# Layer 0 of a two-layer block: shift weights loaded first, the gate turned within the first group, a rotary product ahead of the turns, and all experts' inputs turned first at the end

## The chip, the cores and the metric

The kernel runs on one core of one Trainium2 chip. Its time is the device time of one execution in microseconds (us), as the median of several runs. A profile is one further execution, recorded by the hardware. The core has five engines, each with an instruction queue of its own that is worked off in order: TensorE (PE) for matrix products and transposes, VectorE (DVE), ScalarE (ACT), GpSimd (POOL), and SyncE (SP), which here only issues DMA transfers. POOL and ACT issue a few transfers too. PEld in the profile is the loading of TensorE's stationary operand.

## The reference

Two transformer layers with adaptive layer norm over 1024 tokens of width 512, all in float32. In layer 0 the vector `c` gives six rows by one product, `silu(c) @ wmod`: shift, scale and gate for the attention (rows 0, 1, 2) and for the feed-forward part (3, 4, 5). Attention has 32 query heads and 8 key/value heads of width 128, and its weights come as integers with scales:

```python
mod = (_silu(L0_c) @ L0_wmod).reshape(L0_c.shape[0], 6, 1, -1)
ga = (2 * (ga >= 0) - 1) * jnp.maximum(jnp.abs(ga), 0.25)
h = _layernorm(x, axis=-1) * (1 + ca) + sa
x = x + ga * _L0_attn_ref(h, scales_q, ..., qw_o)
...
w = (qw.astype(jnp.float32) - ZERO) * jnp.repeat(scales, GS, axis=0)
q = _apply_rope(q, cos, sin); k = _apply_rope(k, cos, sin)
scores = jnp.einsum('bhqd,bhkd->bhqk', q, k) / math.sqrt(HD)   # causal, softmax
```

A gated feed-forward part with low-rank additions follows. Layer 1 has its own modulation, attention with 32 heads of width 16, and at the end a mixture of 28 rank-8 experts: each token's two best experts by `logits = xf @ gate_W.T` are weighted by a softmax, and their low-rank outputs are added to a dense product.

```python
h = jnp.einsum('nd,erd->ner', xf, lora_A) * (gate_full * SCALING)[:, :, None]
out = xf @ base_W.T + jnp.einsum('ner,eor->no', h, lora_B)
```

## The kernel before

Everything before layer 1, and the kernel's end, is written in a manual schedule: on each engine the instructions stand in the order in which the Python code issues them. Semaphores between engines come from the tiles that an instruction reads and writes. A tile pool has a fixed number of buffers, and an instruction that needs a buffer waits until the one that held it before is through.

**The begin** (lines 428 to 557). SP issues the loads in the order written: `cc` (c as a column), `row` (c broadcast to all partitions), four tiles of `x`, four tiles of scale weights (`wm`), four tiles of shift weights (`wa`, lines 435 to 438), then the first key weights (`wi`, `ws`) and so on. Transfers of 256 KB each are the rule. DVE makes the layer norm's statistics (L444, L445), ACT the root of the variance (`rstd`, L447) behind the Sigmoid of `cc` (L484) and of `row` (L487). DVE multiplies `row` by its Sigmoid (L489), normalizes x to `xn` (L455) and sums the scale by one pass per chunk (`mod_sum`, L135). TensorE multiplies `cc` by `wa` to get the shift as a row (L497), then transposes `xn` (L465) and the row (L505); DVE copies the shift to `mcol` (L507), and DVE and ACT evict the normalized chunks to `hT` (L478, L473).

Then come the projections of key group 0 and of query heads 0 to 3: `project_k`, `project_v` and `project_q`. The rotary step `project_rope` has eight TensorE passes (L219), three DVE products (L225, L227, L228) and one addition on POOL (L232). `ready` dequantizes a loaded weight on DVE (L212), `load` issues the next one's two transfers on SP (L253, L254). Amid these stand the four `mod_sum` passes of the gate and, at the last one, four small steps that clamp it (L141 to L145). The last thing before the group loop is `gate_row`: DVE spreads the gate's column (L150), TensorE turns it (L158), one engine copies it to a row (L83).

Before the loop, products use four PSUM banks, two of `psA[0]` and two of `psA[1]`, and transposes four of `trp`. At `first.close()` all but `psA[0]` go to the scores' pool `sp`, three buffers of two banks. From there on `psum_mm` has two banks.

**The group loop** (lines 624 to 685). Eight groups, and in each eight steps over query tiles in the order 3, 7, 2, 6, 1, 5, 0, 4. A step `u` has four blocks of 32 queries for its four heads. `scores(u, s)` multiplies (L331), masks (L335, L337), takes the maximum (L339) and the exponential on ACT (L341); `normalize` takes the reciprocal (L348) and scales on ACT (L350). `turn_probs(u, b)` turns block b on DVE (L355) and sends four transfers to `pT` (L357), of blocks 0 and 2 from SP, of 1 and 3 from POOL. Block 0 is turned at the end of the step, blocks 1 to 3 in the following step. `context` and `project_o` (L366, L377) of a step run two steps later, as does `residual`, which multiplies by the gate row (L385). `plan` hands each step of group 0 the next group's products as side pieces; `exchange` dequantizes and loads.

**The end** (lines 1408 to 1423). For the last four token tiles: logits, routing on DVE, then steps given as a string: `b` is the dense product of a tile (L1273, eight passes), `t` weights a tile's expert inputs on DVE (`hg`, L1255) and turns them on TensorE (L1263, L1264), with two copies on ACT, and `e` adds the experts' product (L1280, L1281), multiplies by the gate and adds x on DVE (L1283, L1284) and sends the output. Banks come from a pool of seven, `hg` has two buffers, `hgT` five.

## Time and profile before

| | us |
|---|---|
| median of 3 runs | 1865.36 |
| lowest, highest | 1863.69, 1867.35 |
| profiled execution | 1870.42 |
| its span, first to last instruction | 1868.3 |
| PE busy | 1801.9 (96%) |
| DVE busy | 1164.4 (62%) |
| ACT busy | 671.9 (36%) |
| POOL busy | 479.1 (26%) |
| mean granted clock of TensorE | 0.983 |

All times within the profile count from the span's start. A line of a timeline gives start, length, engine, source line, operation, the tile written and the tiles read, the shapes and the number of instructions merged into it; in brackets, how long the engine was idle before and what ended that. A line of the waits gives engine, tile and line, what was waited for, then the total in us, how often, and the longest. In the profile's slices the span is cut into 40 equal parts, and a digit is the busy share in tenths. A line of the stretches gives the stretch, its length, then for PE, PEld, DVE, ACT and POOL the busy time with the number of instructions, and last the granted share of TensorE's clock, the DMA share and GB/s. Matmuls are pipelined and their ends are modelled, so times of single passes are best read from the distance between starts.

### The profile page before, as it was taken

How to read it: one execution, taken by the hardware profiler on the slowest of the kernel's cores; microseconds unless marked ns; L12 is line 12 of the kernel's file. 1: busy time of each engine (PE TensorE's matmuls, PEld its weight loads, DVE VectorE, ACT ScalarE, POOL GpSimd, SP SyncE). 2: the span in 40 equal slices, each digit the busy share in tenths (PEclk: the TensorE clock that was granted, in tenths of full speed). 3: DMA queues.
4: the chain of work that ended last, by engine and by line, in shares of the span. 5: the costliest groups of instructions: out<-in, count | busy, mean ns of one | idle time of the engine just before them, and what ended most of it. 6: DMA issues, size and time to landing. Idle time of an engine off the chain costs nothing.

```text
span 1868.3 us, 22566 instructions
## 1 busy us (share of the span) xinstructions
PE 1801.9 (96%) x6578; PEld 839.3 (45%) x6578; DVE 1164.4 (62%) x2823; ACT 671.9 (36%) x1398; POOL 479.1 (26%) x705
## 2 busy tenths in 40 slices
PE   7989999999999999999999999999999999999998
PEld 4444445444455444455444544444534433333434
DVE  5677685676765767766777772232555777576443
ACT  1144533434434444433435530000114334455531
POOL 1244443444433444433444420001100100000000
PEclk9999999999999999999999999999999989999999
DMA  6154453354543544533545551001000002000000
GB/s 220 56 150 130 126 143 95 92 146 120 137 115 83 131 120 119 158 91 103 134 108 147 144 193 60 0 0 51 1 2 7 6 11 72 4 8 5 8 18 34
DMA packets 87738, 156.39 MB, mean 84 GB/s; under 512 B 25264, under 2 KB 33072, under 8 KB 87616
## 3 DMA queue, kind: packets, MB, share of 16 engines
q1 hardware_dynamic: 70064, 117.00, 21.9%
q0 software_dynamic: 17312, 37.54, 8.4%
q8 instruction: 54, 0.88, 0.2%
q14 instruction: 68, 0.56, 0.1%
q10 hardware_dynamic: 240, 0.41, 0.1%
HBM read 74.90 MB, written 2.36 MB: 41 GB/s over the span
## 4 chain that ended last, share of the span: by engine, by line
PE 71%; DVE 14%; issue 6%; ACT 4%; DMA 2%; POOL 2%; SPq 1%; ACTq 0%; DVEq 0%; POOLq 0%
PE mm L366 9%; PE sc L823 8%; PE sc L331 8%; PE mm L219 7%; PE mm L377 7%; PE sc L1086 6%; PE sc L1039 5%; PE sc L855 4%; PE ctx L1129 4%; DVE pr L355 3%; PE mm L299 3%; PE sc L942 2%; ACT pr L341 2%; ACT pr L350 2%; DVE t L228 2%
## 5 line engine op out<-in xcount | busy, mean ns | idle before, releaser
L341 ACT ACTIVATE pr<-sc,nb 128x512 f32<-128x512 f32 (+7 forms) x256 | 189.1, 739 | 508.6 <-DVE nb L339 390.6
L219 PE MATMUL mm<-hT,wf 128*128 128x512 f32 x640 | 294.1, 604 | 10.2 <-DVE t L228 7.3
L357 POOL DMA_DIRECT2D pT<-pr x509 | 251.1, 500 | 146.9 <-DMA pT<-pr 43.1
L331 PE MATMUL sc<-kT,qT 128*128 128x512 f32 (+15 forms) x768 | 264.3, 468 | 3.8 <-ACT pr L341 3.0
L366 PE MATMUL mm<-pT,v 128*128 128x512 f32 x576 | 258.8, 594 | 2.8 <-DVE gu L585 1.6
L355 DVE STREAM_TRANSPOSE pr<-pr 128x512 f32<-128x512 f32 (+7 forms) x256 | 189.2, 760 | 82.4 <-ACT pr L350 75.7
L377 PE MATMUL mm<-wo,ctxT 128*128 128x512 f32 x512 | 230.7, 593 | 2.5 <-ACT ctxT L372 1.4
L1086 PE MATMUL sc<-q,kv 32*128 32x512 f32 (+3 forms) x768 | 212.0, 556 | 7.2 <-DVE mx L1049 7.2
L331 PEld LDWEIGHTS sc<-kT,qT 128*128 128x128 f32 x768 | 142.1, 191 | 160.1 <-issue 144.5
L350 ACT ACTIVATE pr<-pr,rs 128x512 f32<-128x512 f32 (+7 forms) x256 | 190.8, 765 | 8.3 <-DVE rs L348 8.3
L219 PEld LDWEIGHTS mm<-hT,wf 128*128 128x128 f32 x640 | 120.1, 193 | 149.4 <-issue 123.0
L339 DVE TENSOR_REDUCE nb<-sc 128x1 f32<-128x416 f32 (+31 forms) x256 | 181.1, 708 | 8.8
L1102 ACT ACTIVATE pspace<-sc 128x512 f32<-128x512 f32 (+3 forms) x303 | 132.3, 495 | 150.0 <-PE sc L1095 110.9
L1039 PE MATMUL sc<-kv,q 32*128 32x512 f32 (+3 forms) x768 | 171.7, 547 | 6.2 <-ACT kv L994 3.0
L386 POOL TENSOR_TENSOR x<-x,ot 128x512 f32<-128x512 f32 x62 | 78.5, 1265 | 345.8 <-DVE ot L385 271.3
L366 PEld LDWEIGHTS mm<-pT,v 128*128 128x128 f32 x576 | 107.7, 190 | 122.0 <-issue 113.3
L1049 DVE CUSTOM_DVE_ANT_0 q<-sc,cwide 128x128 f32<-128x128 f32 (+3 forms) x256 | 125.6, 491 | 52.3 <-PE sc L1039 28.2
L823 PE MATMUL sc<-hT,gu 128*128 128x512 f32 x352 | 153.3, 594 | 0.9 <-DVE ot L385 0.9
L377 PEld LDWEIGHTS mm<-wo,ctxT 128*128 128x128 f32 x512 | 95.9, 190 | 109.1 <-issue 100.9
L1086 PEld LDWEIGHTS sc<-q,kv 32*128 32x128 f32 x768 | 76.8, 191 | 96.4 <-ACT pspace L1102 33.9
L232 POOL TENSOR_TENSOR qT<-t,t 128x512 f32<-128x512 f32 x64 | 86.7, 1355 | 112.1 <-DVE t L228 111.7
L823 PEld LDWEIGHTS sc<-hT,gu 128*128 128x128 f32 x352 | 66.1, 190 | 86.4 <-issue 81.6
(195 smaller groups left out, 1831.2 us busy)
## 6 DMA issues: line engine op xcount, KB each, us to landing
wm<-in_wmodT_dram SPq DMA_DIRECT2D x44, 256.0 KB
wi<-in_qw_q_dram SPq DMA_DIRECT2D x32, 256.0 KB
ws<-in_s_q_dram SPq DMA_DIRECT2D x32, 256.0 KB
wi<-in_qw_o_dram SPq DMA_DIRECT2D x32, 256.0 KB
ws<-in_s_o_dram SPq DMA_DIRECT2D x32, 256.0 KB
pT<-pr SPq DMA_DIRECT2D x64, 128.0 KB
pT<-pr POOLq DMA_DIRECT2D x64, 128.0 KB, 3.2
pT<-pr SPq DMA_DIRECT2D x64, 112.0 KB
```

The costliest lines, as they stand in the source:

```text
L219: nc.tensor.matmul(ps, lhsT=wf[:, c, :], rhs=hT[half][:, c, :], start=(c == 0), stop=(c == NC - 1),)
L331: nc.tensor.matmul(ps[:, n0 : n0 + w], lhsT=q, rhs=kT[u.g][:, n0 : n0 + w], start=True, stop=True)
L339: nc.vector.tensor_reduce(nb, ps[:, : d0 + B], AX.X, ALU.max, negate=True)
L341: nc.scalar.activation(u.pr[:, :, :, s, :].rearrange("p j k i -> p k j i"), ps[:, :nk].rearrange("p (k j i) -> p k j i", j=NB, i=B), AF.Ex ...
L350: nc.scalar.activation(pr, pr, AF.Copy, scale=u.rs[s])
L355: nc.vector.transpose(t, t)
L357: queues[(REP * b + r) % len(queues)].dma_start(u.pT[b * B : (b + 1) * B, r, :, :, :].rearrange("p k s i -> p (k s i)"), t[r * B : (r + 1) ...
L366: nc.tensor.matmul(ps, lhsT=vv[u.g][:, kj, :], rhs=u.pT[:, :, kj, :, :], start=(kj == 0), stop=(kj == u.n - 1),)
L377: nc.tensor.matmul(ps, lhsT=u.ctxT[:, r, :], rhs=wo[u.g][:, r, :], start=(r == 0), stop=(r == REP - 1),)
L823: nc.tensor.matmul(ps, lhsT=w[:, m, c, :], rhs=hTc[b][:, c, :], start=(c == 0), stop=(c == NC - 1),)
L1039: nc.tensor.matmul(ps[:, at : at + w], lhsT=u.q[kp, bass.ts(i, P)], rhs=kT1[kp, u.g, n0 : n0 + w], start=True, stop=True,)
L1086: nc.tensor.matmul(ps[:, : QW - q0], lhsT=kT1[kp, u.g, bass.ts(kb, P)], rhs=u.q[kp, q0:QW], start=True, stop=kb < 4 * u.Q,)
```

## The change

In the begin, the four loads of shift weights are issued ahead of x, and `row` behind x. The last two gate sums and the clamp move behind the last query product; the query products go in the order q(2,0), q(3,0), q(2,1), q(3,1), and the dequantization of q3 with the load of q5 ahead of them. The gate's row is no longer made before the loop. Its column is spread at the end of step (0, 0), into a buffer of the loop's own pool, and turned and copied in step (0, 1), in a bank of `psum_mm`. Step (0, 1) does not turn its block 0 at its end: step (0, 2) does that, together with block 1, behind its first side piece, which is the product and rotary step of head 5's first half. At the kernel's end all four turns stand ahead of all four expert products.

```diff
         nc.sync.dma_start(cc, a["c0"])
-        row = const.tile([P, D], F32, tag="crow", name="crow")
-        nc.sync.dma_start(row, a["crow0"].partition_broadcast(P))
-        load_x(0)
-        scales = [mod_load(0, 1, c) for c in range(NC)]
         wa = []
         for k in range(NC):
             wa.append(fp.tile([P, D], F32, tag=f"wa{k}", name=f"wa{k}"))
             nc.sync.dma_start(wa[k], a["wmodS"][bass.ts(k, P), :])
+        load_x(0)
+        row = const.tile([P, D], F32, tag="crow", name="crow")
+        nc.sync.dma_start(row, a["crow0"].partition_broadcast(P))
+        scales = [mod_load(0, 1, c) for c in range(NC)]
...
             mod_sum(0, 2, c, gate[c])
-        project_q(2, 0)
         ready("q", 3)
         load("q", 5)
-        for c in range(2, NC):
-            mod_sum(0, 2, c, gate[c])
+        project_q(2, 0)
+        project_q(3, 0)
         project_q(2, 1)
-        project_q(3, 0)
         ready("k", 1)
         load("o", 0, 0)
         project_q(3, 1)
-        gate_row(0, 2, lambda: trp.tile([P, 512], F32, tag="tr", name="tr"))
+        for c in range(2, NC):
+            mod_sum(0, 2, c, gate[c])
         first.close()
...
+        spread = []
...
-                turn_prev(1)
-                piece()
+                if (g, i) == (0, 2):
+                    piece()
+                    turn_prev(0)
+                    turn_prev(1)
+                else:
+                    turn_prev(1)
+                    piece()
                 scores(u, 1)
+                if (g, i) == (0, 1):
+                    gate_row(0, 2, psum_mm, spread[0])
                 normalize(u, 0)
...
-                for b in range(NB if (g, i) == (NKV - 2, NT - 1) else 1):
+                if (g, i) == (0, 0):
+                    spread.append(gate_spread(0, 2))
+                for b in range(NB if (g, i) == (NKV - 2, NT - 1) else 0 if (g, i) == (0, 1) else 1):
                     turn_probs(u, b, queues)
...
-    for step in "b4 b5 t4 b6 t5 e4 b7 t6 e5 t7 e6 e7".split():
+    for step in "b4 b5 t4 b6 t5 t6 b7 t7 e4 e5 e6 e7".split():
```

## The prediction

> **What bounds the kernel now.** I read the page first: TensorE (PE) is busy 96% of the span, and its low tenths stand only at both ends, which are what the change touches.

> ```profile
> PE   7989999999999999999999999999999999999998
> PEclk9999999999999999999999999999999989999999
> ```

> Next, what PE waits for in the first 220 us. Four waits carry it: 12.3 us for the shift weights, 3.4 and 0.8 us around the gate row, 5.5 us for a rotary product's last DVE step.

> ```profile
> PE mm L497 <- DMA wa<-in_wmodS_dram: 12.3, 1, 12.3
> PE mm L219 <- DVE t L228: 5.9, 2, 5.5
> PE tr L158 <- DVE spread L150: 3.4, 1, 3.4
> PE sc L331 <- ACT gate L83: 0.8, 1, 0.8
> PE mm L219 <- DVE wf L212: 0.5, 1, 0.5
> ```

> Third, the timeline of the begin: PE's first product starts when wa lands, runs at half rate (6.57 us, eight passes, where eight later take 3.43), and holds the transposes until 18.77. DVE was through with xn at 13.4 and with the scales at 15.8.

> ```profile
> 6.05 0.63 ACT L487 ACTIVATE rsig<-crow 128x512 f32<-128x512 f32 x1 [3.43 <-DMA crow<-in_crow_dram]
> 6.74 2.35 SPq L438 DMA_DIRECT2D wa<-in_wmodS_dram  x4
> 12.28 6.57 PE L497 MATMUL mm<-wa,cc 128*1 128x512 f32 x8 [12.28 <-DMA wa<-in_wmodS_dram]
> ```

> Fourth, the timeline of the end: the last turn's DVE step (hg) stands behind expert 5's output (eo), PE idles 1.81 us, and what follows runs at half rate (0.85 us a pass instead of 0.43).

> ```profile
> 1856.94 0.69 DVE L1284 TENSOR_TENSOR eo<-eo,x 128x512 f32<-128x512 f32 x1
> 1857.55 0.39 DVE L1255 TENSOR_TENSOR hg<-ha,oh 128x224 f32<-128x224 f32 x1
> 1857.99 0.43 PE L1263 MATMUL sc<-ident,hg 128*128 128x128 f32 x1 [1.81 <-DVE hg L1255]
> ```

> Last, granted clock (third figure from the right) by 2 us stretches: each idle spell is followed by 3 to 7 us at 0.50.

> ```profile
> 80.00:82.00 2.00, 2.00 (x3) 0.76 (x3) 0.93 (x3) 0.18 (x1) 0.00 (x0) 0.50 0.00 0
> 84.00:86.00 2.00, 2.00 (x7) 0.91 (x6) 0.51 (x1) 0.00 (x0) 0.00 (x0) 1.00 0.00 0
> ...
> 120.00:122.00 2.00, 2.00 (x3) 0.67 (x2) 2.00 (x3) 1.14 (x4) 0.39 (x1) 0.50 0.35 109
> ```

> Between these places PE runs without a break (22.8 to 59.2, 80.6 to 112.9, 118.6 to 162), so a gain made early is kept.

> **The change, part by part**

> **Load order.** No bytes are added. SP keeps eight transfers in flight: from 6.05 us on one of 256 KB lands each 0.68 us (crow 6.05, x 6.72 to 8.76, wm 9.42 to 11.47, wa 12.14 to 14.17). If the slow first landing belongs to the start, not to crow, the new order lands wa at 6.05 to 8.1, x at 8.8 to 10.8, crow at 11.5, wm at 12.1 to 14.2. PE's first product then ends near 12.5 and leaves the path. But ACT's Sigmoid of crow stands ahead of the layer norm's root: 11.5 + 0.63 + table load 1.28 + 0.30 gives rstd at 13.7 (10.4 before). Then on DVE the reciprocal 0.2, four xn at 0.48: 15.9; four mod_sums at 0.62: 18.4; then the copy of the shift, which was at 21.11. The first projection starts 2.7 us earlier, at 20.05. If crow was what made the first landing slow (an isolated 256 KB row load, 46.50 to 49.11, took 2.6 us), all is up to 2.4 us earlier: 5.1. Against this, PE now idles from the transposes (about 16.8) to 20.05, and every spell of 1.8 us or more in this trace cooled the clock; half rate for 3.4 us costs 1.7. Bounds -1 to +5; I take **+1.5**, nearest to the row with the cold start taken off. Up to 59.18 PE has no other wait.

> **Gate into group 0, products reordered** (times as before, less the start's gain). DVE: rotary of q(1,1) to 61.4, two mod_sums to 63.78 (the second 1.75 because POOL's add runs beside it), dequant of q3 to 64.5. PE idles 62.6 to 64.55, then q(3,0), q(2,1), q(3,1) at 3.44 each: 74.9. DVE: rotaries at 2.1 behind each, the last to 77.05, then the two mod_sums (0.69 + 1.75 less overlap) and four small steps at 0.2: 80.1; now the first scores' mask and maximum (0.95): 81.1, where before they ended at 81.8. PE no longer waits for the gate: scores at 74.9 instead of 78.92, project_k(1,0) by 79.3 instead of 85.4 (0.50 clock). So DVE takes its rotary at 81.1, not 85.5, and the row-for-row rest of step (0,0) reaches its turn at 91.4 instead of 95.47: **4.05**. The spread copy (0.43) fits in DVE's 1.06 us wait for ACT before that turn. The four gate transposes cost 0.45 warm; their copy (0.58) on ACT is beside DVE work. They take one of the two "mm" banks, so q(4,1) must wait for the rotary of q(4,0), to 96.2: PE idles 2.1 us, but DVE wants q(4,1) only at 102.4.

> Moved DMAs: q5's load is issued 2 us earlier, with nothing behind it on SP; o(0,0) still follows k1's dequant. Hidden.

> **The product ahead of the turns.** Before, in (0,2), DVE waited until 113.31 for ACT, turned twice (to 116.6), then did q(5,0)'s rotary, to 118.57, for which PE's q(5,1) waited. After (less 4.05): scores' maximum to 108.0, rotary to 110.05 in what were idle 1.26 + 1.91 us, turns to 112.5. PE runs q(5,1) at 110.1 (118.62 before). Then project_o waits for wo's dequant behind the other turns: 117.05 to 120.5, before 125.67 to 129.1. The sum of both parts is **8.4** at that point. POOL's add now precedes block 1's four pT issues: it ends near 111.8, the turn at 112.5, so nothing waits. SP's four issues of block 0 come after the rotary: by SP's 1.07 us each the eight end near 120, land by 122.5; context(0,1) wants them at 123.4. That cover is 0.9 us; without it PE waits that much.

> Less cooling: new PE idles of 1.9, 2.1 and 3.05 us. The clock's records in the trace change only on a grid of 3.41 us; steps of it that were 45% busy (the end) and 18% busy (before 76.3) cooled the clock, one 69% busy did not. So an idle cools if over 1.88 us of it fall into one step: by where the grid may fall about 0.45, 0.5 and 0.8. A spell costs 1.7 to 3.4; less what DVE's slack hides I take 2.2, 0.7 and 2.0: 1.0 + 0.3 + 1.6 = 2.9. Bounds 0 and 7 (all three, two steps in the first and last); **+5.5** remains.

> [...]

> **The end.** Same instructions. Turn 5 ends at 1849.08; hg6 needs only turn 4 (done 1845.4), so t6 0.22, b7 3.43, t7 0.22: 1852.95; four experts at 1.72: 1859.8, before 1863.56. DVE's 1.4 us an expert is covered by PE's 1.72 until the last, whose tail is the same. **+3.7**: 1.8 of idling, 1.9 of cold clock. Bounds 1.8 (the clock cools elsewhere) and 3.8. What was eo ahead of hg is now later by 3.8 for e4; only its output transfer follows.

> **Sum.** 1.5 + 5.5 + 3.7 = 10.7. Against the profiled execution (1870.42, span 1868.3): 1859.7. That one lies 5.1 above the median, 1865.36; on the median 10.7 off gives **1854.7**.

> **The rivals**

> *No cooling in the new gaps.* 2.7 + 8.4 + 3.7 = 14.8: 1850.6. For it: the gaps are each under the grid's step. Against: 1856 to 1858. [...] Chance 0.17.

> *The begin gives nothing.* Crow's Sigmoid holds rstd longer or the clock stays cold for two steps: -1 instead of 1.5, 1857.2. For it: crow is now ninth of the big loads; against: scales still end by 18.4. Chance 0.15.

> *Group 0 gives its lead back* to the pT transfers (PE waited 0.45 us for one at 162): only the end counts, 1861.7. Against: the turns that feed them move as early as PE does. Chance 0.11.

> *Slower:* the clock's records have six half-rate stretches in layer 1, from 1397 to 1619, 44 us in all, which cost 22. A shifted program meets the grid otherwise; each further 3.41 us window costs 1.7, so from 7 more on the gain is gone; at nine, 1870.0. For it: these stretches follow short idles that may fall either way. Against: the three runs, each with its own grid, lie within 3.7 us. Chance 0.07.

> **How the numbers follow.** Likeliest 0.50 (own range 1851 to 1858), then 0.17, 0.15, 0.11, 0.07. Faster by over 0.2% (under 1861.6; about what a measurement can tell) is 0.50 + 0.17 + 0.15 and 0.04 of the fourth: 0.86; the fourth's rest and 0.02 of the last: 0.09 same; 0.05 slower. The range 1849 to 1862 leaves out the last case and the far end of the second.

> **What would show it.** Right: L497 starting before 7 us, rstd near 13.7, the first L219 near 20; no PE wait for spread or gate; q(5,1) without the 5.5 us wait; the end's PE unbroken from 1831 to the last expert. Wrong: crow landing after 14, a PE wait for hg or for a bank at t7, long 0.50 clock from 94 to 125, or more half-rate stretches in layer 1.

## The result and the profile after

| | before | after |
|---|---|---|
| median, us (14 executions each) | 1865.87 | 1857.26 |
| lowest, highest | 1858.21, 1870.6 | 1849.93, 1864.84 |
| profiled execution, us | 1870.42 | 1857.40 |
| its span | 1868.3 | 1855.3 |
| mean granted clock | 0.983 | 0.984 |

The changed kernel takes 0.9954 of the time before, 95% interval 0.994 to 0.9969: 8.6 us less (5.8 to 11.2). The two profiled executions differ by 13.0 us. That is not the size of the change: executions of one and the same kernel spread over 12 to 15 us. This spread goes with the clock: in the 14 executions of after the mean granted clock runs from 0.980 in the longest to 0.988 in the shortest, and time and clock correlate at -0.98 (-0.93 to -0.98 in every other group of nine or more executions). Which waits move the clock is part of what follows.

After the change, lines behind line 430 of the kernel carry numbers up to 9 higher: hg is L1264, its turn L1272 and L1273, the experts' product L1289 and L1290.

TensorE's slices and clock on the page of after:

```profile
PE   7989999999999999999999999999989999999998
PEclk8999999999999999999999999999999999999999
```

What PE waits for in the first 220 us of after (engine, tile and line, what it waited for, total in us, how often, longest):

```profile
PE mm L497 <- DMA wa<-in_wmodS_dram: 4.1, 1, 4.1
PE tr L465 <- DVE xn L455: 4.0, 1, 4.0
PE mm L366 <- DVE nb L339: 3.5, 1, 3.5
PE mm L219 <- DVE t L228: 2.3, 2, 1.9
PE mm L219 <- DVE wf L212: 1.8, 1, 1.8
PE mm L219 <- DVE hT L478: 1.7, 1, 1.7
```

Of the four waits of before, the 12.3 us for wa are down to 4.1, and the others are gone (3.4 and 0.8 at the gate's row, 5.5 for t). New ones stand elsewhere: 4.0 before the transposes, 1.8 for the dequantized q3 (wf), 1.9 for a bank (t), and 3.5 in front of a context product (L366). The timeline of PE in after shows where they lie:

```profile
4.12 6.33 PE L497 MATMUL mm<-wa,cc 128*1 128x512 f32 x8 [4.12 <-DMA wa<-in_wmodS_dram]
14.40 3.65 PE L465 MATMUL tr<-ident,xn 128*128 128x128 f32 x16 [3.96 <-DVE xn L455]
20.25 5.19 PE L219 MATMUL mm<-hT,wf 128*128 128x512 f32 x8 [1.69 <-DVE hT L478]
...
95.21 3.70 PE L219 MATMUL mm<-hT,wf 128*128 128x512 f32 x8 [1.87 <-DVE t L228]
...
109.16 3.70 PE L219 MATMUL mm<-hT,wf 128*128 128x512 f32 x8
...
114.13 3.70 PE L377 MATMUL mm<-wo,ctxT 128*128 128x512 f32 x8 [0.62 <-ACT ctxT L372]
...
124.03 7.10 PE L366 MATMUL mm<-pT,v 128*128 128x512 f32 x16 [3.46 <-DVE nb L339]
```

The first projection starts at 20.25 (22.77 before) and then takes 5.19 us instead of 3.67: it runs partly at half rate (granted clock 0.79 from 20 to 28 us). The product of head 5's second half, which waited for the rotary step of the first, runs at 109.16 (118.62 before). At 124.03 PE starts on the context of step (0,1), 0.87 us behind the landing of its last transfer of pT at 123.16. In all eight profiles with the product ahead, this distance is 0.83 to 0.87 us; so it is the transfer that the 3.46 us of idling belong to. The name nb is only that of the release seen last: in three of the eight, PE starts before the nb step at that place has ended. These are issues of pT on SP and the last ones on POOL, and from the view of the tile pT the shortest, median and longest time from issue to landing:

```profile
110.41 5.64 SPq L357 DMA_DIRECT2D pT<-pr  x8
...
115.02 1.93 POOL L357 DMA_DIRECT2D pT<-pr  x4 [1.01 <-DVE pr L355]
...
DMA to landing us min/median/max: 1.8/2.7/6.7
```

The end on PE's timeline of after has no wait for hg, and one expert's two halves take 1.02 us each:

```profile
1843.32 0.27 PE L1272 MATMUL sc<-ident,hg 128*128 128x128 f32 x1
1843.53 1.02 PE L1289 MATMUL sc<-eb,hgT 128*128 128x512 f32 x2
...
1849.56 1.02 PE L1290 MATMUL sc<-eb,hgT 96*128 96x512 f32 x2
```

**The lead.** To see where the time went, each of TensorE's passes is matched with the pass of the same place in the trace of before. The difference of the two starts is the lead there, in us. All leads below are against the one trace of before. "Begin" is the first projections, "gate" the mean over the passes at 89 to 95 us of after, where the lead falls from 6.6 to 4.1 at the wait for the bank, "ahead" those just before the context of (0,1), "context" those just behind it.

| profile | begin (56 us) | gate | ahead | context | end of layer 0 | start of layer 1 | 1740 us | 1834 us | span |
|---|---|---|---|---|---|---|---|---|---|
| after | 1.01 | 5.63 | 11.28 | 7.58 | 8.30 | 8.16 | 10.96 | 9.26 | 13.0 |
| after, again | -0.57 | 4.07 | 9.23 | 4.43 | 4.76 | 4.99 | 7.86 | 6.16 | 9.8 |
| end alone | 1.01 | 1.86 | 1.82 | 1.82 | 2.19 | 2.52 | 12.33 | 12.32 | 16.0 |
| begin alone | 2.59 | 3.45 | 3.44 | 3.44 | 3.59 | 3.62 | 6.12 | 1.48 | 3.2 |
| gate alone | 0.98 | 5.62 | 5.14 | 5.14 | 5.35 | 4.59 | 7.44 | 5.74 | 5.7 |
| product ahead alone | 0.23 | 0.17 | 6.27 | 3.01 | 3.19 | 3.33 | 6.05 | 1.55 | 3.2 |

Three things are read from it. The kernels with the old begin (rows 3, 5, 6) also have up to 1.0 us there, so a lead of 1 us at 56 us is no gain. Between the start of layer 1 and 1834 us no instruction differs in any of these kernels, and yet the lead moves by -2.1 to +9.8 us there. And the last column less the one before it is what the end gave: 3.6 to 3.7 with the new end; with the old one 0 in gate alone, and 1.7 in begin alone and in product ahead alone.

### The profile page after: what moved, and what is told of

Same layout as the page of the kernel before. It is cut to its first block, busy times and chain, and to the rows that moved or that the text cites. A ratio compares the mean times of both kernels' runs of the same rounds, so it can differ in the third digit from the quotient of the medians.

```text
span 1855.3 us, 22570 instructions
## 1 busy us (share of the span) xinstructions
PE 1798.5 (97%) x6578; PEld 838.6 (45%) x6578; DVE 1163.8 (63%) x2823; ACT 671.3 (36%) x1398; POOL 478.8 (26%) x705
## 4 chain that ended last, share of the span: by engine, by line
PE 72%; DVE 15%; ACT 5%; issue 5%; DMA 2%; POOL 1%; SPq 1%; ACTq 0%; DVEq 0%; POOLq 0%
PE mm L366 9%; PE sc L331 8%; PE sc L832 8%; PE mm L219 7%; PE mm L377 7%; PE sc L1095 6%; PE sc L1048 5%; PE sc L864 4%; PE ctx L1138 4%; DVE pr L355 3%; PE mm L299 3%; PE sc L951 2%; ACT pr L341 2%; ACT pr L350 2%; PE sc L1282 2%
## 5 line engine op out<-in xcount | busy, mean ns | idle before, releaser
L219 PE MATMUL mm<-hT,wf 128*128 128x512 f32 x640 | 291.6, 600 | 8.0 <-DVE t L228 3.7
L331 PE MATMUL sc<-kT,qT 128*128 128x512 f32 (+15 forms) x768 | 265.5, 469 | 3.4 <-ACT pr L341 3.4
L366 PE MATMUL mm<-pT,v 128*128 128x512 f32 x576 | 258.7, 594 | 4.6 <-DVE nb L339 3.5
L331 PEld LDWEIGHTS sc<-kT,qT 128*128 128x128 f32 x768 | 142.5, 191 | 160.7 <-issue 144.5
L1111 ACT ACTIVATE pspace<-sc 128x512 f32<-128x512 f32 (+3 forms) x303 | 132.2, 495 | 147.5 <-PE sc L1104 108.0
L219 PEld LDWEIGHTS mm<-hT,wf 128*128 128x128 f32 x640 | 119.0, 191 | 145.5 <-issue 119.4
L366 PEld LDWEIGHTS mm<-pT,v 128*128 128x128 f32 x576 | 107.7, 190 | 123.6 <-issue 112.9
```

The source lines that it names most:

```text
L219: nc.tensor.matmul(ps, lhsT=wf[:, c, :], rhs=hT[half][:, c, :], start=(c == 0), stop=(c == NC - 1),)
L331: nc.tensor.matmul(ps[:, n0 : n0 + w], lhsT=q, rhs=kT[u.g][:, n0 : n0 + w], start=True, stop=True)
L366: nc.tensor.matmul(ps, lhsT=vv[u.g][:, kj, :], rhs=u.pT[:, :, kj, :, :], start=(kj == 0), stop=(kj == u.n - 1),)
```

## The experiments

**The four parts, each alone on the kernel before.** The first changes only the end's string:

```diff
-    for step in "b4 b5 t4 b6 t5 e4 b7 t6 e5 t7 e6 e7".split():
+    for step in "b4 b5 t4 b6 t5 t6 b7 t7 e4 e5 e6 e7".split():
```

> The kernel before with the end's new order alone. My theory: by trace, the distance from the first matmul of turn 4 to the span's end shrinks by 3.7 us, 1.8 of idling and 1.9 of half-rate clock; where the kernel before happens not to cool in that 1.81 us gap, by 1.8. Median time 1.8 to 3.7 us less. Rival (bunching: four outputs in a row delay the last transfer): under 1.8 us.

Measured: 0.9979 of the time before (0.9962 to 0.9997), which is 3.9 us less (0.6 to 7.1); the median is 1858.24, beside 1864.11 for the kernel before, measured along with it. The last turns and the experts stand on PE as in after, without a gap and at full rate:

```profile
1840.25 0.27 PE L1263 MATMUL sc<-ident,hg 128*128 128x128 f32 x1
...
1846.49 1.02 PE L1281 MATMUL sc<-eb,hgT 96*128 96x512 f32 x2
```

From 1834 us to the end this profile gains 3.72 us (16.04 less 12.32). The forecast's 3.7 holds against this trace of before. Most of the rest of its 16 us was gained in layer 1, where it had 20.5 us of half-rate clock and the trace of before 44.

The second has the new order of loads alone.

```diff
-        row = const.tile([P, D], F32, tag="crow", name="crow")
-        nc.sync.dma_start(row, a["crow0"].partition_broadcast(P))
-        load_x(0)
-        scales = [mod_load(0, 1, c) for c in range(NC)]
         wa = []
...
             nc.sync.dma_start(wa[k], a["wmodS"][bass.ts(k, P), :])
+        load_x(0)
+        row = const.tile([P, D], F32, tag="crow", name="crow")
+        nc.sync.dma_start(row, a["crow0"].partition_broadcast(P))
+        scales = [mod_load(0, 1, c) for c in range(NC)]
```

> The kernel before with the load order of the begin alone. My theory: first L219 near 20.2 us (22.77 before), at half rate for most of its eight passes, lead of 1.0 us left at 30 us and kept to the end of layer 0; time about 1 us less, inside what a measurement tells. Rival (DVE takes the lead back at the gate, since it is the slow engine from 59 to 77): lead 0 by the first scores.

Measured: 1.0007 (0.9992 to 1.0022), so between 1.5 us less and 4.1 us more: no gain that can be measured. In its profile the begin did gain 2.6 us, for here the first projection found the clock warm (1.00 from 20 to 28 us, 0.79 in after):

```profile
20.17 3.67 PE L219 MATMUL mm<-hT,wf 128*128 128x512 f32 x8 [1.69 <-DVE hT L478]
```

The same wait of 1.69 us, the same start within 0.1 us as in after, but 3.67 us instead of 5.19. This run showed something else: its end is the old one, with the same gap of 1.81 us, and there the clock did not fall. PE's timeline at its end, where the two halves take 1.02 us as in the new end:

```profile
1856.51 0.33 PE L1263 MATMUL sc<-ident,hg 128*128 128x128 f32 x1 [1.81 <-DVE hg L1255]
1856.78 1.02 PE L1280 MATMUL sc<-eb,hgT 128*128 128x512 f32 x2
1857.64 1.02 PE L1281 MATMUL sc<-eb,hgT 96*128 96x512 f32 x2
```

The stretches around that gap (the clock is the third figure from the right), first in begin alone:

```profile
1852.00:1860.00 8.00, 6.19 (x18) 2.54 (x16) 2.95 (x5) 0.85 (x4) 0.00 (x0) 1.00 0.12 48
```

and in before:

```profile
1854.00:1862.00 8.00, 6.19 (x14) 2.75 (x13) 1.81 (x4) 0.85 (x4) 0.00 (x0) 0.79 0.08 33
```

The same 6.19 us busy in 8, the same gap; the clock was 1.00 in the one and 0.79 in the other. Of the four profiles with the old end, two cooled (before, gate alone) and two did not (begin alone, product ahead alone). By this row what the new end is worth depends on the execution: 3.7 where the old one would have cooled, about 2.0 where not.

The third has the gate's part alone: the query products in the new order, the gate's last sums behind them, its row turned in step (0,1). The order of the turns of (0,1) and (0,2), the loads and the end are those of before.

```diff
+                if (g, i) == (0, 1):
+                    gate_row(0, 2, psum_mm, spread[0])
                 normalize(u, 0)
...
+                if (g, i) == (0, 0):
+                    spread.append(gate_spread(0, 2))
```

> The kernel before with the query products reordered, the gate's sums last and its turn in step (0, 1), without the product ahead of the turns. My theory: turn of step (0, 0) at 91.3 us instead of 95.47, PE still waits some 5 us for q(5,0)'s rotary and cools, lead at the context of step (0, 1) and at the end of layer 0 about 4.2 us. Rival (the bank that the gate row takes costs PE what the gate gave): lead under 2 us there.

Measured: 0.9974 (0.996 to 0.9989), 4.8 us less (2.1 to 7.5). Its lead grows from 0.98 at 56 us to 5.14 behind the turns: 4.16, where the prediction had 4.05. The waits of PE in its first 220 us:

```profile
PE mm L219 <- DVE t L228: 6.6, 3, 4.3
PE mm L219 <- DVE wf L212: 1.8, 1, 1.8
```

The gate's waits are gone, the one for q3's weights is as in after, and the old wait for head 5's rotary is still there, 4.3 us now.

The fourth has the product ahead of the turns alone.

```diff
-                turn_prev(1)
-                piece()
+                if (g, i) == (0, 2):
+                    piece()
+                    turn_prev(0)
+                    turn_prev(1)
+                else:
+                    turn_prev(1)
+                    piece()
```

> The kernel before with the product ahead of the turns alone. My theory: q(5,1) starts near 114.2 us (118.62 before), PE does not cool there, context of step (0, 1) starts 4 to 4.6 us earlier than 131.85, held then by PE and no longer by a transfer; alone it gains more than the 3.1 us that it gave in the whole change, where the pT transfers limit it. Rival (it only gives what the transfers allow): 3 us or less here too.

Measured: 1.0006 (0.9989 to 1.0023), between 2.1 us less and 4.3 us more. In its profile the lead is 6.3 us ahead of the context of (0,1) and 3.0 behind it. Its waits of PE:

```profile
PE mm L366 <- DMA ws<-in_s_q_dram: 3.0, 1, 3.0
PE mm L219 <- DVE t L228: 1.6, 2, 1.2
```

The 5.5 us wait has become one of 1.2, and 3.0 are paid again at L366. The trace names the load of q's scales (ws) there, because it landed at the same moment; the last pT of that context lands at 127.77, and PE starts at 128.60. The expectation of 4 to 4.6 us left behind the context falls, and its rival, that the transfers allow no more than 3, holds. That the time shows nothing at all, while the profile shows 3.2 us up to layer 1, has a possible reason in the same profile: it has no half-rate stretch at 113 to 125, where before and the three runs above with the old turns each have one of 6.8 us. Nor did the new wait of 3.0 us cool the clock there (1.00 from 124 to 132 us), as one of 2.93 us did in the second profile of the changed kernel; an execution in which it does would keep less. This was not separated further.

**The changed kernel once more**, without an edit, beside the next runs.

> The changed kernel as it is. My theory: the work is the same, only the clock differs: by trace a lead of about 8 us at the end of layer 0 over the kernel before, less what cools in the gaps of 1.8 to 1.9 us at 62 and 93 us, and then in layer 1 half-rate stretches that move the lead by several us either way. Rival (the clock falls at the same places in every execution): the same cold stretches as in the first profile of the changed kernel.

Measured: 0.9961 (0.9945 to 0.9978), 7.3 us less; median 1858.68. Its profile is the second row of the table: the same waits, but the begin has no lead left and group 0 keeps 5.3 us. PE's timeline in this execution, to be laid beside that of after:

```profile
20.27 6.74 PE L219 MATMUL mm<-hT,wf 128*128 128x512 f32 x8 [1.69 <-DVE hT L478]
...
96.77 5.40 PE L219 MATMUL mm<-hT,wf 128*128 128x512 f32 x8 [1.87 <-DVE t L228]
...
125.55 8.74 PE L366 MATMUL mm<-pT,v 128*128 128x512 f32 x16 [2.93 <-DVE nb L339]
```

Waits of 1.69, 1.87 and 2.93 us; the products behind them take 6.74, 5.40 and 8.74 us, where at full rate they take 3.67, 3.70 and 7.10. In after the wait of 1.87 and the longer one of 3.46 us did not cool the clock. The stretches behind them, first in after:

```profile
96.00:100.00 4.00, 4.00 (x10) 1.71 (x9) 3.96 (x9) 2.73 (x4) 3.02 (x6) 1.00 0.35 82
124.00:128.00 4.00, 3.97 (x10) 1.85 (x11) 3.92 (x10) 3.08 (x5) 2.62 (x6) 1.00 0.49 140
```

and in the second profile of the same kernel:

```profile
96.00:100.00 4.00, 3.23 (x6) 1.45 (x7) 3.91 (x9) 1.64 (x4) 3.02 (x6) 0.76 0.31 70
124.00:128.00 4.00, 2.45 (x3) 1.17 (x4) 3.83 (x11) 1.68 (x3) 2.71 (x4) 0.68 0.70 227
```

So one kernel with one set of gaps has both outcomes, and the rival, the same cold stretches each time, falls. The gap of 1.83 us for q3, which the expectation named too, cooled in neither.

**The row earlier.** Is the begin held by crow, whose Sigmoid stands on ACT ahead of the layer norm's root?

```diff
-        load_x(0)
         row = const.tile([P, D], F32, tag="crow", name="crow")
         nc.sync.dma_start(row, a["crow0"].partition_broadcast(P))
+        load_x(0)
```

> The changed kernel with c's broadcast row loaded behind the shift weights and ahead of x. My theory (rstd waits on ACT behind the Sigmoid of that row): rstd near 12.1 us instead of 13.17, the shift's copy near 17.5 instead of 18.60, first projection 1.1 us earlier, so about 1.1 us more lead at 30 us than the changed kernel with the same clock. Rival (x lands as much later as the row lands earlier, and the statistics end as late): no gain.

Measured: 0.9958 (0.994 to 0.9976), not told apart from the changed kernel. ACT's timeline in after shows what the row does there:

```profile
11.23 0.63 ACT L487 ACTIVATE rsig<-crow 128x512 f32<-128x512 f32 x1 [8.61 <-DMA crow<-in_crow_dram]
11.87 1.28 ACT L447 ACT_TABLE_LOAD   x1
13.17 0.30 ACT L447 ACTIVATE rstd<-mv,eps_t 128x4 f32<-128x4 f32 x1
```

With the row ahead of x, the timeline of ACT and of DVE gives:

```profile
8.83 0.63 ACT L487 ACTIVATE rsig<-crow 128x512 f32<-128x512 f32 x1 [6.17 <-DMA crow<-in_crow_dram]
...
13.48 0.30 ACT L447 ACTIVATE rstd<-mv,eps_t 128x4 f32<-128x4 f32 x1 [2.73 <-DVE mv L445]
...
9.53 0.69 DVE L444 BATCH_NORM_STATS2 bnst<-x 128x6 f32<-128x512 f32 x1 [6.68 <-DMA x<-in_x_dram]
```

The Sigmoid runs 2.4 us earlier, and rstd at 13.48, 0.3 later: now it waits for the statistics of x (mv), whose loads are one place further back. The row and x end together in the changed order, so that bringing the one forward gives nothing.

**Keeping the clock.** Six products are added in the begin, four behind the shift's row and two ahead of the copy to `mcol`. They multiply the identity by wa into a bank whose content nobody reads.

```diff
+        def keep_warm(n):
+            for k in range(n):
+                nc.tensor.matmul(idle, lhsT=ident, rhs=wa[k % NC], start=True, stop=True)
...
+        keep_warm(4)
         banks = ln_transposes(xn)
...
+        keep_warm(2)
         nc.vector.tensor_copy(mod[0, 0], ps[:, :NC])
```

> The changed kernel with six added products on TensorE whose results nobody reads, four ahead of the transposes of xn and two behind those of the shift row, to keep the clock up. My theory (the begin's gain is spent on the cold clock): transposes end 1.7 us earlier, the first projection's eight passes take 3.5 us instead of 5.2, lead at 30 us 2 us or more above the changed kernel's. Rival (DVE and the loads set the begin): no more than 0.6 us.

Measured: 0.9954 (0.9935 to 0.9972), median 1856.84; the interval holds the changed kernel's ratio. In the profile, PE's timeline of the begin, where L487 of PE is the added products:

```profile
9.45 3.70 PE L487 MATMUL mm<-wa,ident 128*128 128x512 f32 x8
14.61 2.03 PE L465 MATMUL tr<-ident,xn 128*128 128x128 f32 x16 [1.46 <-DVE xn L455]
16.90 1.98 PE L487 MATMUL mm<-wa,ident 128*128 128x512 f32 x4
19.91 3.67 PE L219 MATMUL mm<-hT,wf 128*128 128x512 f32 x8 [1.02 <-DVE hT L478]
```

Its clock from 12 to 20 us:

```profile
12.00:20.00 8.00, 5.52 (x28) 2.99 (x27) 7.01 (x20) 3.12 (x6) 0.00 (x0) 1.00 1.04 376
```

and that of after:

```profile
12.00:20.00 8.00, 4.16 (x20) 3.77 (x20) 6.51 (x17) 2.50 (x5) 0.00 (x0) 0.57 1.05 372
```

The transposes take 2.03 us (3.65 in after), the first projection 3.67. The lead at 56 us is 2.86, so 1.9 more than in after and 3.4 more than in its second profile. This shows what ate the begin's gain: the half-rate clock behind the new idle spells. The eight profiles with wa ahead line up by it: with no half-rate record in the begin the lead at 56 us is 2.9 and 2.7, with 3.4 us of it 2.6, with 6.8 us 0.9, with 10.2 us 1.0 and 0.2, with 13.7 us -0.6 and -1.0. The other executions point the same way: the mean granted clock is 0.9864 here and 0.9842 to 0.9845 in the three other variants of the changed kernel measured along with it, and 0.9826 in begin alone, beside 0.9859 for the kernel before.

**The loads out of the way of pT.** SP issues the loads of step (0,2) among pT's transfers. The first attempt moved their place in the code behind `normalize(u, 3)`:

```diff
-                    for w in come:
-                        load(*w)
+                    if (g, i) != (0, 2):
+                        for w in come:
+                            load(*w)
...
                 normalize(u, 3)
+                if (g, i) == (0, 2):
+                    for w in come:
+                        load(*w)
```

> The changed kernel with the four weight transfers of step (0, 2) issued at the step's end instead of in its middle. My theory (context of step (0, 1) waits for the last pT transfers, which share the engines with these loads): last of them lands 0.7 to 1.3 us earlier than 123.16, PE's 3.5 us wait shrinks by as much, and the lead at the end of layer 0 grows by it. Rival (the late loads make a dequantization of step (0, 3) late): the lead there is smaller than the changed kernel's.

Measured: 0.9966 (0.9948 to 0.9983). The attempt tells nothing of its question: between the two places SP issues nothing else, so its queue is in the same order as in after, the loads still come right behind the issues of pT, and the last of those takes 6.6 us from issue to landing (6.7 in after). The run counts as one more of the changed kernel; from 56 us to the end of layer 0 it gained 4.9 us.

The second attempt moved them behind the step's own `turn_probs`, so that four more transfers of pT go first.

```diff
                     turn_probs(u, b, queues)
+                if (g, i) == (0, 2):
+                    for w in come:
+                        load(*w)
```

> The changed kernel with the four weight transfers of step (0, 2) issued behind that step's own first four pT transfers, some 8 us later (the run with the loads at the step's end had left SP's order as it was). My theory (these loads share the engines with the last pT transfers): from the issue of the first pT transfer of step (0, 1) to the landing of the last takes 11.5 to 12 us instead of 12.7, PE's wait of 2.9 to 3.5 us ahead of the context shrinks by 0.7 to 1.2. Rival (the pT transfers are slow by themselves): 12.5 us or more, wait unchanged.

Measured: 0.9963 (0.9946 to 0.998). The sixteen transfers of pT for (0,1) now land in 11.6 us from the first issue to the last landing (111.18 to 122.80), where after has 12.75 (110.41 to 123.16). PE's waits:

```profile
PE mm L366 <- DVE sc L337: 2.3, 1, 2.3
PE mm L366 <- DVE ot L385: 1.5, 1, 1.5
```

The first context waits 2.3 us instead of 3.5; the following one now waits 1.5 us, and the lead falls from 8.0 at 133 us to 6.1 at the end of layer 0. What was won at one context was lost at the next.

**Both** of these, the six products and the loads behind:

> The changed kernel with the six added products that keep the clock up in the begin and with the loads of the run beside it. My theory: the two add up, lead over the kernel before at the end of layer 0 some 9.7 us where the group's gaps do not cool and 7 to 8 us where they do, plus what the loads give; time 1 to 3 us below the changed kernel, hardly told by a measurement. Rival: the loads take back what the clock gives.

Measured: 0.9945 (0.9925 to 0.9964), median 1855.32 from six executions. It is the lowest median of all, and its interval and that of the changed kernel (0.994 to 0.9969) overlap almost wholly, so it isn't shown to be faster. Its profile has the shortest span, 1848.4, with a lead of 8.6 at the end of layer 0 and 19.4 at 1740 us. The six products alone had 9.7 at the end of layer 0, with no half-rate record in group 0, where this profile has one of 3.4 us; that the two parts add up is not shown. From the start of layer 1 to 1740 us 9.8 us more were gained, without a changed instruction. The stretch of layer 1 that holds these, in before:

```profile
1380.00:1630.00 250.00, 240.58 (x1514) 100.25 (x1514) 163.48 (x473) 95.95 (x221) 20.10 (x17) 0.91 0.07 19
```

in after:

```profile
1380.00:1630.00 250.00, 240.44 (x1567) 99.31 (x1565) 163.55 (x470) 101.29 (x235) 20.14 (x17) 0.92 0.07 19
```

and in this kernel:

```profile
1380.00:1630.00 250.00, 240.45 (x1623) 99.43 (x1625) 171.16 (x483) 106.75 (x245) 20.13 (x17) 0.96 0.07 19
```

PE is busy as long in all three, but the clock is 0.91, 0.92 and 0.96. The counts of instructions rise with it, though the stretch starts at another place of the program in each. Half-rate records in layer 1 add up to 44 us in before, 37.5 in after, begin alone and others, and 20.5 in end alone and here.

## Why the prediction was right, and where it was not

The time came out 2.6 us above the forecast, inside the likeliest case's own range (1851 to 1858), and faster, as expected. The sum of 10.7 us was too large by about 2.1; the terms were not all right.

**Begin, +1.5: it gave nothing.** The landings were as reckoned or better: L497 starts at 4.12, since the first load lands at 4.1 when it is wa, against 6.05 when it was crow (so the start was not what made that landing slow); crow lands at 11.20, rstd runs at 13.17 (13.7 predicted), the first L219 at 20.25 (20.05). Earlier by 2.5 us, that is, as the sum had it. What failed is the price of the clock. The sum took one half-rate window, 1.7 us, off a lead between 2.7 and 5.1 us. In the profiles the lead at 56 us is 1.0, -0.6, -1.0 and 0.2 in four executions of this begin and 2.6 in the run with the begin alone, 0.45 on average, against 0, 1.0, 1.0 and 0.2, 0.55 on average, with the old begin. The half-rate record is 10.2 us long in after and 13.65 in its second profile. Six products in the gaps bring the lead to 2.86, and over the eight profiles it falls with the length of the half-rate record, so the cause is shown. The rival "the begin gives nothing" named this, a clock cold for two steps or more, and its 1857.2 is the nearest of all to the measured 1857.26. It was right on the begin, though it was offered for crow's Sigmoid just as much, and that was not it.

**Group 0, 8.4 at the point where both parts meet, 5.5 kept.** The gate's part was right: the turn of (0,0) runs at 90.29 in after instead of 95.47, which is 5.18 less the begin's 1.0, and 4.16 alone; predicted 4.05. Two of the three idle spells came where they were said to, 1.8 for q3 (1.9) and 1.87 for the bank (2.1). The third, 3.05 us ahead of the output product, did not: that product waits 0.6 us for ctxT at 114.13 and not for wo, and PE is free for the context at 120.57.

The product ahead of the turns ran as said (109.16; 110.1 predicted), but one step was mis-sized. The prediction gave the context of (0,1) a cover of 0.9 us over the landing of pT at 122.5. They land at 123.16, and PE, earlier than reckoned, stood waiting for 3.46 us. The reason given there, SP's 1.07 us per issue, was not the limit: SP's eight issues were through at 116.05, not near 120. The sixteen transfers of 128 KB take some 0.65 us each, 10.4 to 10.7 us from the first packet to the last (9.6 with the loads behind). Before, this was hidden: the last landed at 128.42 and PE came at 131.68, which leaves 2.4 us of slack beyond the 0.85 us from landing to start. So this part is worth 2.8 us alone, not 4.35, and the lead behind that context is 7.6 in after instead of 8.4 and the begin's gain on top. Of the rival in which the transfers take group 0's lead back, about a third came true: 3.7 of 11.3 us.

The 5.5 us kept came out as a mean, but partly by luck. In after none of the gaps cooled the clock (7.3 us kept from 56 us to the end of layer 0), in its second profile two did (5.3). The three other kernels with the same group 0 kept 6.9 (the six products, none cooled), 4.9 (the loads' first attempt, two) and 3.8 (the row earlier, two). The mean of the five is 5.6. The mechanism was there, but cooling cost some 1.5 us on average, not 2.9: without it 7.1 were kept, not 8.4, and the difference is what was lost to the pT transfers, for which the sum had nothing. The two errors nearly cancel. One correction: the old group 0 varies too. It gained 1.2 and 1.0 us in end alone and begin alone against this trace of before, so that before's profile was a cold one there. Against the mean of these three the gain is 4.9.

Gaps of 1.81, 1.87 and 2.93 us, all under the grid's step, cooled the clock in these profiles, and the place of the grid of 3.41 us against the kernel differs from one execution to the next. The rival of no cooling is what the profile of after shows in group 0, by luck of its grid; the second profile of the same kernel refutes it as a rule. The prediction's own rule, more than 1.88 us of idling in one step, is near what the profiles show, with a zone from 1.8 to 2.0 where either happens. The step at the end of before from which it was read was busy for 1.60 of 3.41 us, 47% and not 45%, and held a gap of 1.81 us.

**End, +3.7: right against this trace, too large on average.** From 1834 us on the new end gains 3.1 to 3.75 us, 3.6 on average, in all eight profiles that have it. The step that failed is the certainty given to the old end: the prediction let a gap fall on either side of the grid in group 0, but took the 1.81 us at the end to cool always, since it had in the one trace at hand. It did in two profiles of four; the other two lose 1.7 us less. In all four the gap lies whole within one step of the grid, so its 1.81 us are within the zone where either happens. Against the mean of the four the end gives about 2.8. The trace at hand held the warning. The prediction says that every spell of 1.8 us or more in it cooled the clock, but 63 us ahead of that gap the same line waits for 2.93 us, and behind it the clock stays at 1.00. PE's timeline and the stretch in before:

```profile
1795.00 0.33 PE L1263 MATMUL sc<-ident,hg 128*128 128x128 f32 x1 [2.93 <-DVE hg L1255]
...
1795.00:1799.00 4.00, 4.00 (x11) 1.99 (x12) 0.00 (x0) 1.71 (x3) 0.00 (x0) 1.00 0.14 33
```

The grid cuts this gap to 1.15 and 1.78. In after, one step holds 2.88 of the same 2.93 us, and the clock from 1784 to 1788 is 0.57. It fell at this gap in ten of the twelve profiles, all but before and end alone.

**The sum again:** 0 for the begin, 4.9 for group 0 and 2.8 for the end are 7.7 us, inside the measured 5.8 to 11.2. The parts alone, by time, give -1.3 for the begin, 4.8 for the gate, -1.1 for the product ahead and 3.9 for the end: 6.3, each uncertain by some 3 us. The rest, up to 8.6, can't be assigned: it lies within these uncertainties and is less than the lead moves behind the start of layer 1 without a changed instruction (-2.1 to +9.8 us).

**Slower through layer 1.** The rival's mechanism is real, and works in both directions: half-rate time of 20.5 to 44 us for the same instructions. The prediction doubted it because three executions lay within 3.7 us; fourteen lie within 12.4. It moves single executions, and profiles, and it had no measurable sign for the kernel as a whole. Not every stretch there follows an idle, as the prediction has it: in before PE is busy throughout from 1606 to 1612 us, the clock falls at 1612.3, and all twelve profiles have this stretch. Why stays open. The shortest two profiles, end alone and the last experiment, had their grid 1.96 us after the start of layer 1, the others at 0.5 to 0.7, 1.0 to 1.4 or 3.3; this was only seen, not tested.

**Left open.** Whether the six added products and the later loads make the kernel faster than the changed one can't be told by these times. Whether pT's transfers can be made to land faster than with the loads behind them (9.6 us) was not tried; for the product ahead of the turns they are what limits.

## What to carry to other kernels

Time won by starting earlier can go again where TensorE idles in between: here the first projection started 2.5 us earlier, and the lead at 56 us was 1.0 and -0.6 in two profiles of the changed kernel, 2.86 with six products in the gaps. Where a changed order opens a gap of 1.8 us or more, price the half-rate clock behind it too, and try a few products whose result nobody reads. In these twelve profiles, from 55 to 150 us and from 1750 us on, 2.1 us or more of idling within one step of the grid always cooled the clock (18 of 18) and 1.8 to 2.0 did so in a third of the cases (six of 18). Where a gap fell on the grid differed from one execution to the next (the grid stood 0.5 to 3.3 us behind the start of layer 1), so a profile shows one throw; give old gaps the same chance as new ones, and size a part from several profiles. When a product is moved ahead, count the transfers that feed the next consumer from first issue to last landing, for they need not move as early as the engine does: here PE came to the context 11.1 us earlier (120.57 instead of 131.68), and the last of them landed 5.3 us earlier (123.16 instead of 128.42).

## What was not expected of the hardware

Two things. The same 1.81 us gap, in stretches with the same 6.19 us of work in 8, gave a granted clock of 1.00 and of 0.79, and one kernel's executions spread over 12 to 15 us of 1860 for such reasons, with two profiles of equal layer-1 work at 20.5 and 44 us of half-rate clock. And once cold, the clock came back only slowly in the half-busy begin: from 12 to 20 us PE was busy for 4.16 us of 8, and the half-rate record lasted 10.2 us in one execution and 13.65 in another.
